# One fused AdaLN layer on one core: set-up reordered, and the slots of the first block rearranged

## The chip, the core and the metric

The kernel runs on 1 core of one Trainium2 chip. A core has five engines with instruction streams of their own: TensorE (PE; its weight loads are PEld), VectorE (DVE), ScalarE (ACT), GpSimd (POOL) and SyncE (SP), which here issues most of the DMA transfers. An engine runs its own instructions in the order in which they are written, and waits on semaphores where an operand comes from another engine or from a transfer. The issue of a transfer is an instruction of such a stream as well: when it has to wait, everything written behind it on that engine waits too.

The metric is device time in microseconds of one execution, the median of several runs.

## The reference

A batch of B = 4 sequences of T = 2048 tokens with D = 512 channels goes through one layer with two halves. Each half is an adaptive layer norm, an operation and a gated residual:

```python
mod = (silu(c) @ wmod).reshape(B, 6, 1, -1)          # sa, ca, ga, sb, cb, gb per sequence
h = layernorm(x) * (1 + ca) + sa
x = x + ga * attn(h)
h = layernorm(x) * (1 + cb) + sb
x = x + gb * ffn(h)
```

`attn` is a damped oscillator with gates that depend on the token. From h come omega (softplus), zeta (sigmoid) and a force F; the state of 2 x 64 numbers then follows a linear recurrence over the 2048 tokens, and the output is `xs @ C.T + h @ D_mat.T`:

```python
z_new = d_t * (S_t * z - DT * A_t * S_t * y)         # A = omega**2, S = 1/(1 + DT**2 A), d = 1 - zeta
y_new = d_t * (DT * S_t * z + S_t * y)
x_new = concatenate([z_new, y_new]) + F_t
```

`ffn` mixes each token with the one before it and has a receptance, a key and a value product, each 512 x 512:

```python
xr = mu_r * x + (1 - mu_r) * x_prev;  xk = mu_k * x + (1 - mu_k) * x_prev
out = sigmoid(xr @ W_r.T) * (square(relu(xk @ W_k.T)) @ W_v.T)
```

All is float32.

## The kernel before

**Units, blocks, slots.** The tokens are cut into pieces of 256 tokens of one sequence: 32 units, numbered so that unit i has block s = i // 4 and sequence b = i % 4. Units 0 to 3 are the first block, one piece of each sequence. Each unit has two halves. `gts[i]` is the gate half: statistics of the raw tokens, the product with the gate weights (`project`), and the delivery of the gates into the maps of its block. `scan(s)` is VectorE's recurrence over the four units of a block; it is a list of steps with costs, and `take(n)` in the program's text emits steps of it up to n microseconds. Its result, the states y, goes by DMA from the maps to a tile of another layout (L414). `fin[i]` is the finish half: the direct product with D and the product with the states (`attend`), the layer norm of the result (`normalize`), transposes and the token mix (`mix`), and then `key`, `receptance` and `value`.

The loop over `fin` (L1203) has one slot per unit. A slot finishes unit i, prepares unit i + 1 (`ahead`) and does gate work of units i + 9 and i + 10. Slots 0 to 3 are written one way (L1206 to L1269), all later ones another way, which the change leaves alone.

**A gate unit's norm.** For units from 4 on, ScalarE computes mean and variance with accumulating activations (`norm`, L187 and L193), GpSimd makes 1/std and std (L197 to L199), `send` writes these 2 KB from SBUF to DRAM (L203, each partition holds 4 numbers), `spread` reads one row back as a broadcast to 128 partitions (L214), and `multiply` (L258, VectorE) scales the projected gates by it. `deliver` then writes them to the maps on ScalarE (L273) and, with `share`, on VectorE (L271). `spread` can be issued only when the write of `send` has landed. Up to gts[7] both are issued by GpSimd, from gts[8] on by SyncE.

**Set-up (L1028 to L1187).** The weights are specialised per sequence: gate weights, and for each sequence b a D matrix scaled by columns: a TensorE product called a pick (`scale_rows`, L122) spreads one row over all partitions, VectorE multiplies it with D into `dg[:, b]` (`d_scaled`, L966), ScalarE scales by rows (`Turn.rows`, L979), TensorE transposes (`Turn.turn`, L988), ScalarE copies it back (`Turn.keep`, L992), and SyncE stores it to DRAM for the later blocks (L798). Before that, `dg[:, 2]` holds the transposed tokens of gts[4] and gts[5], `dg[:, 3]` those of gts[6] and gts[7], so `d_scaled(2)` and `d_scaled(3)` must follow these projects. `fin[b].products()` (L470, L484) forms the direct product of the first block ahead of time and parks it. The steps of `scan(0)` stand between all these on VectorE.

**Buffers that matter.** The raw tokens of the gate units go through a ring of three tiles (`xs`, L159): the second tile of gts[5] takes the first one of gts[4], so its load waits until norm(4) has read it; likewise the second of gts[9] waits for norm(8). The tokens of gts[6] and gts[7] lie in `wr` until the receptance weights are loaded there, `px` is a ring of three PSUM tiles, `pm` and `pt` have two each. `made_early` and `raw_gates` are parts of `wvb`, the place of the value weights.

The order of everything around the change is the order of the program's text: no scheduler moves instructions.

Of the kernel before, what the change touches and what calls it, by code (L numbers as in the profile page):

```python
# [21 lines left out]
P = 128  # L22
# [28 lines left out]
def adaln_layer_kernel(ctx: ExitStack, tc: tile.TileContext, x, x_t, c_t, wmod, w_gate, w_b, b_gate, b_f, c_mat, d_mat,  # L51
# [223 lines left out]
    def scan(s):  # L275
# [123 lines left out]
        def by_batch(q):  # L399


            if q == 0:
                y_of[s] = p2.tile([P, B, W], F32, tag="y", name=f"y_{s}")
            t = [whole[:, i, 1, ts(q, W)] for i in range(2)]
            for i in range(2):
                there = t[i].rearrange("p (c l) -> p l c", l=L)
                if s == 0:
                    nc.scalar.copy(there, parts[:, i, 0, :, q, :])
                else:
                    std = env["std"][:, ts(q, W)].rearrange("p (c l) -> p l c", l=L)  # L410
                    nc.vector.tensor_mul(there, parts[:, i, 0, :, q, :], std)
            for r in range(2):
                for i in range(2):
                    (nc.sync if s else nc.scalar).dma_start(y_of[s][ts(i, M), 2 * q + r, :], t[i][ts(r, M), :])  # L414
# [17 lines left out]
    class Finish:  # L432
# [148 lines left out]
        def mix(self, between):  # L581
            xn, b = self.xn, self.u.b
            mixed = self.mixed = p1.tile([P, 2, KC, W], F32, tag="mixed", name=f"mixed_{self.tag}")
            edge = p2.tile([P, 2, KC], F32, tag="edge", name=f"edge_{self.tag}")
            if self.u.s == 0:
                nc.gpsimd.tensor_copy(edge, first_f[:, b])
            else:
                nc.gpsimd.tensor_tensor(
                    edge, prev_f[:, b], carry[:, b, :].unsqueeze(1).broadcast_to([P, 2, KC]), ALU.mult
                )  # L590
            pts = []
            for g in range(KC // 2):
                pt = ps2.tile([P, 2, W], F32, tag="pt", name=f"pt_{self.tag}_{g}")
                for j in range(2):
                    for n in range(NT):
                        nc.tensor.transpose(pt[:, j, ts(n, P)], xn[:, n, ts(2 * g + j, P)], ident)  # L596
                pts.append(pt)

            for i in (1, 0):
                for k in (0, 2, 1, 3):  # L600
                    pt, m = pts[k // 2][:, k % 2, :], mixed[:, i, k, :]
                    nc.scalar.activation(  # L602
                        m, pt, AF.Identity, bias=mod[:, SB, k, b : b + 1], scale=now_f[:, b, i, k : k + 1]
                    )
                    nc.vector.scalar_tensor_tensor(  # L605
                        m[:, 1:], pt[:, : W - 1], prev_f[:, b, i, k : k + 1], m[:, 1:], ALU.mult, ALU.add
                    )
                nc.gpsimd.tensor_tensor(mixed[:, i, :, 0], mixed[:, i, :, 0], edge[:, i, :], ALU.add)  # L608
                if i == 1:
                    if self.fast:  # L610
                        self.key_sums()

                        nc.gpsimd.tensor_copy(edge[:, 1, 0:1], self.sums[:, 3, 1, W // 2 - 1 :])
                    between()
            for g, pt in enumerate(pts):
                nc.vector.tensor_copy(carry[:, b, 2 * g : 2 * g + 2], pt[:, :, W - 1])
# [5 lines left out]
        def key(self):  # L622
            mixed = self.mixed
            act = self.act = p1.tile([P, KC, W], F32, tag="act", name=f"act_{self.tag}")
            for e in range(KC // 2):
                pk = ps2.tile([P, 2, W], F32, tag="pm", name=f"pk_{self.tag}_{e}")
                for j in range(2):
                    for k in range(KC):
                        nc.tensor.matmul(
                            pk[:, j, :], wk[:, k, ts(2 * e + j, P)], mixed[:, 1, k, :],  # L630
                            start=(k == 0), stop=(k == KC - 1),
                        )
                nc.scalar.activation(act[:, 2 * e : 2 * e + 2, :], pk, AF.Relu)  # L633
                self.squares(e)
# [63 lines left out]
        def token_quarters(self, which):  # L698
            return [[self.mixed[:, which, 2 * k : 2 * k + 2, ts(t, P)] for t in range(2)] for k in range(2)]
# [35 lines left out]
        def receptance(self):  # L735
            mixed = self.mixed
            self.r = []
            for n in range(NT):
                pr = ps2.tile([P, D], F32, tag="pm", name=f"pr_{self.tag}_{n}")
                for k in range(KC):  # L740
                    nc.tensor.matmul(pr, mixed[:, 0, k, ts(n, P)], wr[:, k, :], start=(k == 0), stop=(k == KC - 1))  # L741
                r = p2.tile([P, D], F32, tag="r", name=f"r_{self.tag}_{n}")
                nc.scalar.activation(r, pr, AF.Sigmoid)
                self.r.append(r)
# [114 lines left out]
    mixed_room = p1.tile([P, 2, KC, W], F32, tag="mixed", name="dt_room")  # L859
    dt = mixed_room.rearrange("p i k w -> p (i k w)").rearrange("p (k n) -> p k n", k=KC)  # L860
    dn, wn = wr, wvb[:, 3]
# [108 lines left out]
    class Turn:  # L970
# [19 lines left out]
        def keep(self):  # L990
            for k in (2, 3, 0, 1):
                nc.scalar.copy(self.dst[:, k, :], self.pts[k])  # L992
            keep_in_dram("dg", self.b)
# [96 lines left out]
    gts[4].project()  # L1090
    for i in (6, 7):
        load_transposed(gts[i].u, gts[i].xt)
    gts[4].load()
    weights_to(wn, w_v, nc.sync)
    weights_to(wk, w_k, nc.sync)
# [8 lines left out]
    rowb = mod_rows(wm_gb, "gb", room=px)  # L1104
    rowc = mod_rows(wm_cb, "cb", room=px)
    gts[4].keep_raw()
    gts[5].project(ps3.tile([P, 2, W], F32, tag="px", name="pg_5"))
    gts[4].norm_means()
# [4 lines left out]
    gts[6].project()  # L1113
    turn_d[0].turn()
    turn_d[0].keep()
    pca = scale_rows(2)
    d_scaled(2, pca)
    take(6)
    turn_d[1].rows()
    row = mod_rows(wm_sb, "sb", room=px)  # L1120
# [7 lines left out]
    gts[4].norm_squares()  # L1128
    gts[4].send(nc.gpsimd)
    gts[7].project()  # L1130
    fin[0].products()
    turn_d[1].turn()
    turn_d[1].keep()
    gts[7].keep_raw()
    pca = scale_rows(3)
    d_scaled(3, pca)
    take(100)
    turn_d[2].rows()
# [6 lines left out]
    gts[4].spread(nc.gpsimd)  # L1145
    fin[1].products()
    turn_d[2].turn()
    turn_d[2].keep()
    gts[8].load_t()
    gts[5].norm()  # L1150
    gts[5].send(nc.gpsimd)
    turn_d[3].rows()
    fin[2].products()
    turn_d[3].turn()
    turn_d[3].keep()
    gts[5].spread(nc.gpsimd)
    gts[9].load_t()
    fin[3].products()
# [6 lines left out]
    fin[1].add_products()  # L1165
    c23 = c_rows(2, made_early[0])
    gts[4].multiply()
    gts[6].norm()
    gts[6].send(nc.gpsimd)
    fin[0].attend(lambda: None)  # L1170
    fin[0].normalize()
    gts[8].project()
    gts[4].deliver(share=1)
    gts[8].keep_raw()
    fin[1].shift(nc.vector)
    gts[6].spread(nc.gpsimd)
    fin[0].mix(lambda: None)
    gts[9].project(ps3.tile([P, 2, W], F32, tag="px", name="pg_9"))
# [24 lines left out]
    for i, f in enumerate(fin):  # L1203
        at = i % B
        ahead = fin[i + 1] if i + 1 < len(fin) else None
        if i < 4:  # L1206
            if i == 3:
                take(100)
            fin[i + 2].load()
            gts[i + 10].load()  # L1210
            f.key()
            if i == 0:
                ahead.attend(lambda: None)
                ahead.stats(NT - 1)
                ahead.norm_factors()
            if i == 0:
                gts[6].multiply()
                gts[6].deliver(share=1)
            else:
                norm_send(i + 9)  # L1220
            if i == 3:
                gates(11)
            take(4 if i == 1 else 6)
            if i == 2:
                sums_s(key_weights, quarters_of(wk, True))
            if i == 3:
                sums_t(receptance_weights, quarters_of(wr))
            if i:
                if not ahead.fast:
                    ahead.add_products()  # L1230
                ahead.attend(lambda: take(2))
                ahead.normalize()
            else:
                ahead.norm_apply()
            if i == 0:
                c_scaled(2, c23)
            if i == 1:
                gts[9].multiply()
                gts[9].deliver()
            value_scaled(i)  # L1240
            if i == 3:
                fetch("dg", i + 3)
            if i == 0:
                gts[7].multiply()
                gts[7].deliver(share=1)
                gts[8].norm()
# [4 lines left out]
            if i:  # L1251
                take(5)
            f.receptance()
            ahead.mix(fin[i + 2].shift)
            if i == 0:
                side += scan(1)
                take(0.1)
                take(0.1)
            if i:
                gts[i + 9].load_t()  # L1260
            gts[i + 9].spread()
            f.value(lambda: take(3 if i == 0 else 4), room=px)
            if i < 3:
                ahead.gate_row = ahead.row(1)
# [3 lines left out]
            if i == 1:  # L1268
                gates(10)  # L1269
        else:  # L1270
# [181 lines left out]
```

## Time and profile before

| | us |
|---|---|
| median of 3 runs | 1159.91 (1157.11 to 1160.78) |
| profiled execution, its own time | 1159.07 |
| its span, first to last instruction | 1157.3 |
| PE busy | 1094.4 (95%) |
| DVE busy | 752.1 (65%) |
| ACT busy | 661.4 (57%) |
| POOL busy | 186.6 (16%) |
| mean granted TensorE clock | 0.979 |

The profile is that of one execution, 1.8 us shorter in span than in time. A page of a profile gives busy time by engine, the span in 40 slices, transfers by queue, the chain of work that ended last, and the costliest groups of instructions. The trace behind it can be asked for waits (who waited for whom, total, times, longest), for the timeline of an engine (start, length, instruction, and in brackets the idle time before it and what ended it), and for busy time by stretch. An "SPq" row is the issue of a transfer by SyncE, not the transfer itself.

Landmarks of the execution: the last step of scan(0) ends at 104.6 us; the states of the first block are multiplied from 117.25; the transposes of units 1, 2 and 3 (L596) start at 152.64, 197.03 and 238.30; the key product of unit 3 ends at 256.5.

### The profile page before, as it was taken

How to read it: one execution, taken by the hardware profiler on the slowest of the kernel's cores; microseconds unless marked ns; L12 is line 12 of the kernel's file. 1: busy time of each engine (PE TensorE's matmuls, PEld its weight loads, DVE VectorE, ACT ScalarE, POOL GpSimd, SP SyncE). 2: the span in 40 equal slices, each digit the busy share in tenths (PEclk: the TensorE clock that was granted, in tenths of full speed). 3: DMA queues.
4: the chain of work that ended last, by engine and by line, in shares of the span. 5: the costliest groups of instructions: out<-in, count | busy, mean ns of one | idle time of the engine just before them, and what ended most of it. 6: DMA issues, size and time to landing. Idle time of an engine off the chain costs nothing.

```text
span 1157.3 us, 14456 instructions
## 1 busy us (share of the span) xinstructions
PE 1094.4 (95%) x4692; PEld 733.2 (63%) x4692; DVE 752.1 (65%) x1824; ACT 661.4 (57%) x1366; POOL 186.6 (16%) x379
## 2 busy tenths in 40 slices
PE   7987867889999999999999999999999999999998
PEld 4753533554677766666667766666666665566666
DVE  5647538846777578765886568755876567664444
ACT  1655665443756476657755576657765565435453
POOL 1111220112121112111111011111111011111110
PEclk8999888889999999999999999999999999999999
DMA  9937225455245754577555754576656753444311
GB/s 312 324 128 174 87 78 99 133 160 161 88 161 158 142 162 128 175 226 152 174 168 162 139 168 132 158 238 136 176 168 168 130 175 137 146 155 136 101 55 37
DMA packets 136835, 176.68 MB, mean 153 GB/s; under 512 B 22828, under 2 KB 94764, under 8 KB 129080
## 3 DMA queue, kind: packets, MB, share of 16 engines
q1 hardware_dynamic: 133112, 173.92, 51.9%
q10 hardware_dynamic: 3328, 1.32, 0.4%
q0 software_dynamic: 320, 0.53, 0.4%
q8 instruction: 37, 0.61, 0.2%
q14 instruction: 38, 0.31, 0.1%
HBM read 146.29 MB, written 25.25 MB: 148 GB/s over the span
## 4 chain that ended last, share of the span: by engine, by line
PE 72%; DMA 12%; ACT 7%; DVE 5%; SPq 2%; issue 1%; POOL 1%; ACTq 0%; DVEq 0%; POOLq 0%
PE pv_c L756 15%; PE pd_c L534 12%; PE pxk_c L659 7%; PE pxr_c L659 6%; PE pg L245 5%; DMA xt<-in_x_t_dram 4%; DMA bc<-st 4%; PE pg L235 4%; PE pzk_c L659 4%; PE pzr_c L659 3%; PE pd_c L492 3%; PE pd_c L470 3%; DMA st<-rs 2%; PE pt_c L596 2%; PE pr_c L741 2%; PE pyk_c L659 2%
## 5 line engine op out<-in xcount | busy, mean ns | idle before, releaser
L756 PE MATMUL pv_c<-wvb,act_c 128*128 128x512 f32 (+1 forms) x528 | 227.5, 584 | 0.0
L534 PE MATMUL pd_c<-dg,xt 128*128 128x512 f32 x432 | 206.2, 593 | 0.0
L605 DVE SCALAR_TENSOR_TENSOR mixed_c<-pt_c,prev_f,mixed_c 128x255 f32<-128x255 f32 x256 | 118.2, 481 | 85.3 <-ACT mixed_c L602 85.3
L756 PEld LDWEIGHTS pv_c<-wvb,act_c 128*128 128x128 f32 x528 | 100.6, 192 | 107.2 <-issue 101.5
L602 ACT ACTIVATE mixed_c<-pt_c,mod,now_f 128x256 f32<-128x256 f32 x256 | 130.5, 560 | 25.5 <-DVE mixed_c L605 19.5
L273 ACT ACTIVATE maps<-g,bias 64x256 f32<-64x256 f32 x112 | 83.2, 742 | 75.0 <-DVE g L258 67.5
L534 PEld LDWEIGHTS pd_c<-dg,xt 128*128 128x128 f32 x432 | 74.5, 191 | 55.9 <-issue 55.0
L245 PE MATMUL pg<-xt,wgb 128*128 128x256 f32 x320 | 85.4, 379 | 0.0
L553 ACT ACTIVATE xn_c<-x 128x512 f32<-128x512 f32 x44 | 27.7, 629 | 93.6 <-DVE x L478 89.7
L659 PEld LDWEIGHTS pxk_c<-dg 128*128 128x128 f32 x448 | 58.7, 191 | 26.1 <-issue 24.1
L478 DVE SCALAR_TENSOR_TENSOR x<-pd_c,rs,x 128x512 f32<-128x512 f32 x56 | 41.7, 745 | 48.5 <-PE pd_c L492 48.4
L463 POOL TENSOR_TENSOR x<-x,row 128x1024 f32<-128x1024 f32 x30 | 70.7, 2355 | 3.3 <-DMA row<-col_rows 3.1
L576 ACT ACTIVATE xn_c<-x,mean_c,var_c 128x512 f32<-128x512 f32 x64 | 48.6, 807 | 29.8 <-POOL mean_c L572 29.7
L245 PEld LDWEIGHTS pg<-xt,wgb 128*128 128x128 f32 x320 | 59.2, 190 | 7.2
L659 PE MATMUL pxk_c<-dg 128*128 128x128 f32 x448 | 59.1, 275 | 0.0
L492 PE MATMUL pd_c<-cg,y 128*128 128x512 f32 x112 | 56.3, 593 | 0.0
L659 PE MATMUL pxr_c<-wvb 128*128 128x256 f32 x208 | 53.4, 379 | 0.0
L741 PE MATMUL pr_c<-wr,mixed_c 128*128 128x512 f32 x96 | 44.4, 618 | 6.5 <-ACT act_c L633 6.1
L596 PE MATMUL pt_c<-ident,xn_c 128*128 128x128 f32 x256 | 36.1, 284 | 13.3 <-ACT xn_c L576 13.3
L608 POOL TENSOR_TENSOR mixed_c<-mixed_c,edge_c 128x4 f32<-128x4 f32 x64 | 13.4, 210 | 218.6 <-ACT mixed_c L602 195.3
L759 DVE TENSOR_TENSOR r_c<-pv_c,r_c 128x512 f32<-128x512 f32 (+1 forms) x66 | 44.0, 666 | 6.5 <-PE pv_c L756 6.4
L677 DVE TENSOR_TENSOR act_c<-act_c,pzk_c 128x256 f32<-128x256 f32 x28 | 11.8, 420 | 54.1 <-PE pzk_c L659 53.9
(254 smaller groups left out, 2027.4 us busy)
## 6 DMA issues: line engine op xcount, KB each, us to landing
dg<-dg SPq DMA_DIRECT2D x30, 1024.0 KB, 7.8
xt<-in_x_t_dram SPq DMA_DIRECT2D x112, 256.0 KB, 7.8
wvb<-wv SPq DMA_DIRECT2D x26, 1024.0 KB, 15.0
x<-in_x_dram SPq DMA_DIRECT2D x32, 512.0 KB, 7.0
out_dram<-r_c SPq DMA_DIRECT2D x62, 256.0 KB, 2.0
xs<-in_x_dram SPq DMA_DIRECT2D x54, 256.0 KB, 12.4
row<-col_rows SPq DMA_DIRECT2D x36, 256.0 KB, 11.6
wvb<-in_wmod_dram SPq DMA_DIRECT2D x5, 1024.0 KB, 8.8
```

Of the source, the lines that this page charges most:

```text
L245: nc.tensor.matmul(self.pg[:, i, :], wgb[:, u.b, k, ts(i, P)], self.xt[:, k, :], start=(k == 0), stop=(k == KC - 1))
L273: nc.scalar.activation(there, here, AF.Identity, scale=sign, bias=bias[src, i, b : b + 1])
L463: engine.tensor_tensor(xt, xt, self.shift_row.unsqueeze(1).broadcast_to([P, NT, D]), ALU.add)
L492: nc.tensor.matmul(pc, y_of[u.s][:, u.b, ts(n, P)], cg[:, u.b, :], start=start, stop=True)
L534: nc.tensor.matmul(pds[n], self.h[:, k, ts(n, P)], dg[:, self.at, k, :], start=(k == 0), stop=False)
L576: nc.scalar.activation(self.xn[:, n, :], self.x[:, n, :], AF.Identity, bias=self.mean[:, n : n + 1], scale=self.var[:, n : n + 1],)
L596: nc.tensor.transpose(pt[:, j, ts(n, P)], xn[:, n, ts(2 * g + j, P)], ident)
L602: nc.scalar.activation(m, pt, AF.Identity, bias=mod[:, SB, k, b : b + 1], scale=now_f[:, b, i, k : k + 1])
L605: nc.vector.scalar_tensor_tensor(m[:, 1:], pt[:, : W - 1], prev_f[:, b, i, k : k + 1], m[:, 1:], ALU.mult, ALU.add)
L659: nc.tensor.matmul(to[:, j, :], left[:, k, ts(j, P)], right[:, k, :], start=start and j == k == 0, stop=(k == 1), skip_group_check=True,)
L741: nc.tensor.matmul(pr, mixed[:, 0, k, ts(n, P)], wr[:, k, :], start=(k == 0), stop=(k == KC - 1))
L756: nc.tensor.matmul(pv, act[:, k, ts(n, P)], wvb[:, self.at, k, at], start=(j == 0), stop=(j == KC - 1))
```

## The change

In the set-up, the picks of sequences 2 and 3 move up behind project(4); the D matrix's other copy `dt` gets its room in `wk`, so the load of the key weights moves behind its use; norm(4) moves from two places (its means ahead of turn 0, its squares behind turn 1's rows) to one place behind turn 2; project(6) and project(7) move to stand behind turn 0, one of them in the PSUM ring px; two of the products move later, products(3) behind unit 0's normalize; the four stores of dg move out of `Turn.keep` to one place behind the scan; norm(6) moves behind the mix of unit 0, ahead of norm(7). Half of the transfers of y in the first block go through SyncE instead of ScalarE.

In slots 0 to 2, attend and normalize of the coming unit come first, then key; the mix is split into `turn` (transposes), `mix_part(1)` (for the key) and `mix_part(0)` (for the receptance) with a tile each, and receptance stands between the two parts; the norm, send and spread of gts[i + 9] (in slot 0 of gts[8] and gts[9]) move behind the second part. Slot 3 keeps its order. The core of the diff:

```diff
-                    (nc.sync if s else nc.scalar).dma_start(y_of[s][ts(i, M), 2 * q + r, :], t[i][ts(r, M), :])
+                    (nc.scalar if s == 0 and r else nc.sync).dma_start(y_of[s][ts(i, M), 2 * q + r, :], t[i][ts(r, M), :])
...
-    dn, wn = wr, wvb[:, 3]
+    dn, dt, wn = wr, wk, wvb[:, 3]
...
         def keep(self):
             for k in (2, 3, 0, 1):
                 nc.scalar.copy(self.dst[:, k, :], self.pts[k])
-            keep_in_dram("dg", self.b)
...
     gts[4].project()
+    pcas = [scale_rows(b) for b in range(2, B)]
     for i in (6, 7):
         load_transposed(gts[i].u, gts[i].xt)
     gts[4].load()
     weights_to(wn, w_v, nc.sync)
-    weights_to(wk, w_k, nc.sync)
     gts[5].load()
...
+    weights_to(wk, w_k, nc.sync)
+    rowb = mod_rows(wm_gb, "gb")
+    rowc = mod_rows(wm_cb, "cb")
     gts[4].keep_raw()
     gts[5].project(ps3.tile([P, 2, W], F32, tag="px", name="pg_5"))
-    gts[4].norm_means()
     turn_d[0].rows()
...
-    gts[6].project()
     turn_d[0].turn()
     turn_d[0].keep()
-    pca = scale_rows(2)
-    d_scaled(2, pca)
+    gts[6].project()
+    d_scaled(2, pcas[0])
     take(6)
+    gts[7].project(ps3.tile([P, 2, W], F32, tag="px", name="pg_7"))
     turn_d[1].rows()
...
-    gts[4].norm_squares()
-    gts[4].send(nc.gpsimd)
-    gts[7].project()
-    fin[0].products()
+    gts[7].keep_raw()
     turn_d[1].turn()
     turn_d[1].keep()
-    gts[7].keep_raw()
-    pca = scale_rows(3)
-    d_scaled(3, pca)
+    d_scaled(3, pcas[1])
     take(100)
+    fin[0].products()
     turn_d[2].rows()
...
-    gts[4].spread(nc.gpsimd)
-    fin[1].products()
     turn_d[2].turn()
     turn_d[2].keep()
+    gts[4].norm()
+    gts[4].send(nc.gpsimd)
+    fin[1].products()
+    turn_d[3].rows()
+    turn_d[3].turn()
+    turn_d[3].keep()
+    gts[4].spread(nc.gpsimd)
     gts[8].load_t()
+    fin[2].products()
     gts[5].norm()
     gts[5].send(nc.gpsimd)
...
     fin[1].add_products()
+    for b in range(B):
+        keep_in_dram("dg", b)
     c23 = c_rows(2, made_early[0])
+    gts[5].spread(nc.gpsimd)
+    gts[9].load_t()
     gts[4].multiply()
+    fin[0].attend(lambda: None)
+    fin[0].normalize()
+    fin[3].products()
+    gts[4].deliver(share=1)
+    gts[8].project()
+    gts[8].keep_raw()
+    fin[1].shift(nc.vector)
+    fin[0].mix(lambda: None)
+    gts[9].project(ps3.tile([P, 2, W], F32, tag="px", name="pg_9"))
     gts[6].norm()
     gts[6].send(nc.gpsimd)
     gts[6].spread(nc.gpsimd)
     gts[7].norm()
     gts[7].send(nc.gpsimd)
```

The slots 0 to 2 after the change, whole:

```python
        if i < 3:
            fin[i + 2].load()
            if i:
                gts[i + 9].load_t()
            gts[i + 10].load()
            if i:
                ahead.add_products()
            ahead.attend(lambda: None)
            ahead.normalize()
            f.key()
            if i == 0:
                gts[6].multiply()
                gts[6].deliver(share=1)
                c_scaled(2, c23)
            if i == 1:
                gts[9].multiply()
                gts[9].deliver()
            if i == 2:
                sums_s(key_weights, quarters_of(wk, True))
            take(6)
            value_scaled(i)
            ahead.turn()
            ahead.mix_part(1)
            f.receptance()
            if i == 0:
                gts[7].multiply()
                gts[7].deliver(share=1)
            take(5)
            ahead.mix_part(0)
            ahead.keep_carry()
            fin[i + 2].shift()
            if i == 0:
                side += scan(1)
                take(0.1)
                take(0.1)
                gts[8].norm()
                gts[8].send()
                gts[8].spread()
                gts[9].norm()
                gts[9].send()
            else:
                norm_send(i + 9)
            gts[i + 9].spread()
            f.value(lambda: take(4), room=px)
            ahead.gate_row = ahead.row(1)
            if i == 0:
                gts[8].multiply()
                gts[8].deliver()
            if i == 1:
                gates(10)
```

## The prediction

> **What bounds the kernel now.** I read the busy table by stretch first, then the waits inside the bad stretch, then the chain and two queues' timelines. Units 0 to 3 are the first block; gts[i] and fin[i] are the gate half and the finish half of unit i. All times are us from the span's start.
>
> ```profile
> 55.00:256.50 201.50, 154.37 (x504) 93.13 (x503) 125.03 (x289) 106.02 (x204) 35.22 (x74) 0.90 0.43 117
> 256.50:1100.00 843.50, 839.68 (x3689) 567.22 (x3688) 565.37 (x1392) 508.37 (x1070) 139.66 (x271) 1.00 0.55 157
> ```
>
> Columns are length, then busy PE, PEld, DVE, ACT, POOL, then granted clock, DMA share, GB/s. From 256.5 on TensorE is busy 839.68 of 843.50, so what arrives late there ends late, and nothing is regained. Before it, from 55, TensorE idles 47 us. The change lives in that stretch; its worth is the change of those 47 us. The waits there:
>
> ```profile
> POOL bc L214 <- DMA st<-rs: 27.9, 3, 12.1
> ...
> DVE dg L966 <- PE pca L122: 19.6, 2, 11.2
> ...
> PE pc_c L492 <- DMA y<-maps: 6.9, 1, 6.9
> ```
>
> VectorE waits 19.6 us for two picks (what the change aims at). GpSimd waits 27.9 us for the 2 KB write of the norm rows. The chain shows one such trip ending in VectorE's multiply:
>
> ```profile
> 137.18 12.41 DMA st<-rs
> ...
> 150.17 4.12 DMA bc<-st
> ...
> 154.38 0.70 DVE g L258
> ```
>
> And SyncE's queue shows it twice more:
>
> ```profile
> 163.54 0.38 SPq L798 DMA_DIRECT2D wv<-wvb  x1
> 164.02 0.39 SPq L203 DMA_DIRECT2D st<-rs  x1
> 177.60 0.32 SPq L214 DMA_DIRECT2D bc<-st  x1
> 178.01 0.39 SPq L203 DMA_DIRECT2D st<-rs  x1
> 187.31 0.32 SPq L214 DMA_DIRECT2D bc<-st  x1
> ```
>
> From issuing the write to issuing the read takes 9.3 us when nothing is ahead (178.01 to 187.31; GpSimd's 121.73 to 131.06 the same) and 13.0 to 13.6 with a 1 MB transfer issued beside it (137.18 to 150.17, 164.02 to 177.60). The read lands 3.6 to 4.6 later. So from norm to multiply a trip costs 1.6 (GpSimd) + 9.3 to 13.6 + about 4 = 15 to 19 us. Today norm(8) ends at 159.2 and its multiply runs at 181.53 unwaited: cover is ample.
>
> **Set-up: what the picks give.** The picks of batches 2 and 3 go early: 2 x 0.95 us of PE after project(4). Then d_scaled(2) waits only for project(5) (it overwrites those columns in dg): cols, rows and project shift 1.9, end 54.8, against 60.7 now. d_scaled(3) needs project(6) and (7), moved directly behind the first turn: 56.5 + 1.65 + 3.5 + 3.5 = 65.1, against 80.66. The remaining scan is unchanged, 82.87 to 104.6 = 21.8 plus the 2.3 of d_scaled, so VectorE ends it near 89 instead of 104.6: 15 earlier. Two queues take that back.
>
> ScalarE: its order is keep(0), rows(1), three copies, keep(1), products(0), rows(2), keep(2), norm(4), products(1), rows(3), keep(3), products(2), norm(5), then the copies of y. With 2.05 a keep, 2.9 a rows, 7.0 of PE per products, 1.65 per turn, 2.75 a norm I get keep(1) to 71.0, products(0) 76.8, keep(2) 83.35, norm(4) 86.1, keep(3) 95.75, products(2) 101.5, norm(5) 104.3. So y is copied at 104.3 against 110.97.
>
> SyncE: the second load of gts[5] waits for norm(4)'s square (a buffer ring of three), as now it blocks the queue from 47.2 to 67.3. norm(4) has moved, so it blocks to 85.5. Behind it stand w_k (moved) and col_rows, 10.0 to the first row read, then rows, and c_rows, 6.3 to landing: 104.9. c_scaled and the three x additions follow, 105 to 109.9, with nothing saved against 104.63 to 109.3. y, half of it now on SyncE, lands near 110; attend(0) starts at 110.2 against 117.25, then products(3) (7.1, moved here) and project(8) run on PE while GpSimd waits for st of gts[5] to 117.5 before unit 0's norm factors. Transposes near 124.5, the mixes of unit 0 end at 130.2 against 132.9 (last mixed L605 and L602). Gain so far: 2.7. The four 1 MB stores of dg, now behind y in one go, plus c_rows and xt of gts[9], are 5 MB: at 340 GB/s (the 80 to 100 stretch's rate at full share) 15 us from 109. That is beside PE's 22 us up to project(9), so nothing; at half that rate project(9) waits 8 us, hidden because the next wait lasts to 161.
>
> **First slot: two trips in series.** gts[6] and gts[7] are normed only after the mix, and GpSimd's order is send(6), spread(6), norm(7), send(7), spread(7), and only then the norm factors of unit 1. norm(6) ends 132.9, send 134.55, spread 147.5 (13.0: w_r's 1 MB goes out beside it, as today), then 0.6 + 1.55, send(7) 149.6, + 9.35 = spread(7) at 159.0, factors to 160.55, xn, unit 1's transposes at 161.6. Today: 152.64. That is 9.0 late, and the receptance of unit 0, which today fills that gap, now stands behind the transposes.
>
> **Slots 1 and 2: the multiply comes straight after its norm.** norm(8) moves from 156.6 to behind both mixes and the softening: transposes 164.1, receptance 7.4 (its first part at the low clock; the page's slices show 8 here) 171.5, sigmoid, gates(7) 1.5, second mix 2.5, Abs to Ln 5.0 = 181.2. SyncE then holds: xs of gts[9] waits for norm(8)'s first square (183.3), the shift row of unit 2 stands behind it and lands at 188.4, and GpSimd shifts x (2.36) before norm(8)'s own small work. send(8) 192.4; between 9.35 and 13.6 I take 11 as wv's 1 MB went 4 us before: spread 203.5, landed 207. On VectorE multiply(8) stands ahead of unit 2's additions and of half of scan(1); it would be reached at 187, so it waits 20. Then 0.7 + 1.2 + 3.6 + GpSimd 1.3 gives unit 2's transposes at 215.1; today 197.03. Late by 18.
>
> Slot 2 repeats it. multiply(9) 217.5, value_scaled(1) to 226.8, first mix 229, three scan steps, second mix 237.2, norm(10) to 239.9, shift, xs and wv ahead, send(10) 241.4, 13.2 (1 MB directly ahead) + 0.3 + 3.6 = 258.5. VectorE would be at multiply(10) at 245.3. Additions to 261.2, ScalarE's gates and statistics to 265.1, GpSimd 1.7, transposes of unit 3 at 267.8; today 238.30. Then receptance 7.4, value 7.1, key 7.1 and the transposes 2.4: key(3) ends 291.8 against 256.5, late by 35.3 (today the receptance ran before the transposes). Last, y of the second block stands on SyncE behind spread(11): 300.5 against TensorE's need at 298.8, 1.7 more. The rest I cost at nothing. Two tiles instead of one add no instruction and free nothing that is waited for. attend ahead of key puts 1.9 us of PE first, but unit 1's factors wait for spread(7) anyway; in return ScalarE reaches key(0)'s relu only after xn, 162.3, beside transposes and receptance, which last to 171.5. The earlier xt loads of gts[10] and gts[11] land long before their projects. mod_rows moves from px to pm in PSUM, whose buffers were emptied at 42. From unit 3 on the order is as before.
>
> Sum: 35.3 + 1.7 = 37.0 later than the profiled execution, whose time is 1159.07 (span 1157.3 + 1.8): 1196.1. That execution is 0.84 below the median of 1159.91, so 1196 to 1197; I say 1196.
>
> The Trainium skill's page "DMA: Bandwidth & Descriptors", section "Anatomy of one DMA — SWDGE (gpsimd) path", gives about 2 us fixed per DMA plus bytes, for this 2 KB write as for any. The rows above show 8.8 to 12.4 us to landing for it, so the rows decide; by the page the four trips below one another would be some 40 us shorter in all and key(3) would end some 3 us earlier than now, 1156 (an estimate from that page). The same page's "Rules for kernel authors" says to issue a DMA early and wait on it late; the changed order does the reverse for gts[8] and gts[10].
>
> **Rivals.**
> - Faster: the trips of gts[8] and gts[10] are hidden, so TensorE runs through from unit 1's transposes at 161.6. Its work to the end of key(3) is 77.6 (transposes 2.4, receptance 7.5, then eight stages of 7.1, project 3.5, two state products of 1.9, two sets of transposes of 1.8), ending 239.2, 17 earlier: 1142. VectorE has 62 us of work there, which fits. It decides if norm to multiply takes under 3 us in slot 1 and under 6 in slot 2; no trip in the trace took under 14.
> - Half: slot 1 waits as worked out, slot 2's trip is covered (a statement order I misread, or a short landing). From 215.1 TensorE needs 52.5: 267.6, 11 late: 1170.
> - Worse: the 5 MB stores are slow, st of gts[5] and gts[6] land 4 to 6 later each, and the later writes all take 13.6: 37 + 9 to 16: 1205 to 1212.
> - The scan still waits: d_scaled(2) for project(5) 2.4, d_scaled(3) for project(7) 1.5. So the aim is met but for 4 us; it moves the total nowhere, since ScalarE and SyncE end later.
>
> **How the numbers follow.** Forecast 0.62, half 0.17, worse 0.13, faster 0.07, no change 0.01. With every write at 9.3 the forecast's own low end is 37 - 3.7 - 1.7 - 3.8 = 28, and with the set-up 5 better 23: its own range is 1182 to 1205. The half rival bounds the range below at 1170, the worse one above at 1212. A difference of 0.3% (3.5 us) is about what these runs can tell from none: slower 0.92, same 0.01, faster 0.07.
>
> **What would show it.** VectorE's wait for picks gone, its scan over near 89, but c_scaled near 105. GpSimd's wait at spread(6) 9 to 13 long, unit 1's transposes near 161. VectorE waiting some 10 to 20 us at L258 for bc, twice; TensorE idle of about 20 us three times before 270, and its total idle from 55 to the steady part about 84 instead of 47. Wrong if the multiplies of gts[8] and gts[10] show no wait, or if unit 2's transposes come before 200.

## The result and the profile after

The changed kernel takes 1201.53 us (median of 4 runs, 1200.39 to 1207.3) against 1158.51 of the kernel before beside it: ratio 1.0382, 95% interval 1.0341 to 1.0423. It is slower, inside the predicted range and 5.5 us above the predicted 1196. The profiled execution took 1200.39 us, 41.3 more than the profiled one of before (1159.07); the sum of the prediction was 37.0.

Busy time by stretch, changed kernel (columns as in the prediction: length, PE, PEld, DVE, ACT, POOL, clock, DMA share, GB/s):

```profile
55.00:288.70 233.70, 151.34 (x520) 93.43 (x519) 127.16 (x289) 107.90 (x212) 36.71 (x75) 0.82 0.38 99
288.70:310.20 21.50, 14.07 (x37) 7.43 (x36) 4.81 (x8) 6.77 (x14) 1.07 (x3) 0.84 0.51 142
310.20:1142.00 831.80, 828.34 (x3655) 560.74 (x3654) 561.34 (x1385) 502.24 (x1057) 137.13 (x269) 1.00 0.55 157
```

The first stretch again ends with the key product of unit 3. TensorE is idle for 82.4 of its 233.7 us, where before it was idle for 47.1 of 201.5. The second runs to the receptance of unit 3, and TensorE is idle for another 7.4 there. From 310.2 on it is busy for 828.3 of 831.8 at a granted clock of 1.00, so nothing of the loss comes back.

The waits of VectorE, TensorE and GpSimd from 55 to 300, changed kernel (total, times, longest):

```profile
PE pt_c L596 <- ACT xn_c L576: 57.9, 7, 25.7
DVE g L258 <- DMA bc<-st: 54.0, 5, 18.5
...
POOL bc L214 <- DMA st<-rs: 41.2, 4, 10.7
...
DVE cg L1006 <- DMA c_rows<-col_rows: 13.4, 1, 13.4
...
PE pg L235 <- DMA xt<-in_x_t_dram: 11.1, 1, 11.1
...
PE pc_c L492 <- DMA y<-maps: 6.7, 1, 6.7
...
DVE dg L973 <- PE pg L235: 3.9, 2, 2.2
```

The 19.6 us that VectorE waited for picks are gone, and 3.9 for `project` came in their place. The new waits are larger: 54.0 for the norm rows at the multiply, where before had one of 5.5, and 13.4 for `c_rows`, which swallows nearly all of the 15 us by which the scan is earlier. TensorE's wait at the transposes for the coming unit's norm rose from 13.3 to 57.9; its wait for y of the first block is as before, 6.7 against 6.9, and the 11.1 for the input of gts[9] come back below.

The chain through one row trip, from four timelines of the changed kernel. SyncE's queue with the rows of gts[8] and gts[9] (their norms are written at the end of slot 0, and they are waited for while TensorE is in slot 1):

```profile
188.59 0.38 SPq L807 DMA_DIRECT2D wv<-wvb  x1
191.71 0.38 SPq L203 DMA_DIRECT2D st<-rs  x1
203.70 0.32 SPq L214 DMA_DIRECT2D bc<-st  x1
204.11 0.39 SPq L203 DMA_DIRECT2D st<-rs  x1
212.67 0.32 SPq L214 DMA_DIRECT2D bc<-st  x1
```

VectorE's multiplies of gts[8], gts[9] and gts[10] (in brackets the idle time before, and what ended it):

```profile
206.62 0.69 DVE L258 TENSOR_TENSOR g<-wvb,bc 128x512 f32<-128x512 f32 x1 [18.52 <-DMA bc<-st]
...
217.68 0.69 DVE L258 TENSOR_TENSOR g<-wvb,bc 128x512 f32<-128x512 f32 x1 [5.70 <-DMA bc<-st]
...
255.12 0.69 DVE L258 TENSOR_TENSOR g<-pg,bc 128x512 f32<-128x512 f32 x1 [9.68 <-DMA bc<-st]
```

And TensorE's first transposes of units 1, 2 and 3:

```profile
162.09 0.47 PE L596 MATMUL pt_c<-ident,xn_c 128*128 128x128 f32 x1 [12.29 <-ACT xn_c L576]
...
213.85 0.47 PE L596 MATMUL pt_c<-ident,xn_c 128*128 128x128 f32 x1 [25.70 <-ACT xn_c L576]
...
264.11 0.47 PE L596 MATMUL pt_c<-ident,xn_c 128*128 128x128 f32 x1 [18.94 <-ACT xn_c L576]
```

GpSimd, ahead of the first row (the shift of unit 2's x):

```profile
188.00 2.34 POOL L463 TENSOR_TENSOR x<-x,row 128x1024 f32<-128x1024 f32 x1 [10.71 <-DMA row<-col_rows]
```

Read them together. The norm of gts[8] ends on ScalarE at 184.6, but its row leaves only 7 us later: GpSimd's small work for it is written behind the shift of unit 2's x, which waits for a transfer of its own. The row of gts[8] leaves at 191.71, SyncE may read it back at 203.70, VectorE has stood for 18.52 us when it lands, and the additions to unit 2's x stand behind that multiply on VectorE. So unit 2 reaches the transposes at 213.85, after TensorE has been idle for 25.70. Unit 3 repeats it with the row of gts[10]. Before, the three sets of transposes started at 152.64, 197.03 and 238.30.

The last part of the loss lies at the second block's states, in SyncE's queue:

```profile
283.05 0.38 SPq L203 DMA_DIRECT2D st<-rs  x1
293.82 0.32 SPq L214 DMA_DIRECT2D bc<-st  x1
294.23 0.86 SPq L771 DMA_DIRECT2D out_dram<-r_c  x2
295.14 0.45 SPq L448 DMA_DIRECT2D row<-col_rows  x1
295.68 7.20 SPq L414 DMA_DIRECT2D y<-maps  x8
```

and on TensorE:

```profile
291.94 3.60 PE L470 MATMUL pd_c<-dg,xt 128*128 128x512 f32 x8
302.96 2.05 PE L492 MATMUL pd_c<-cg,y 128*128 128x512 f32 x2 [7.43 <-DMA y<-maps]
304.80 4.63 PE L470 MATMUL pd_c<-dg,xt 128*128 128x512 f32 x8
```

The eight copies of y are written behind the reading of gts[11]'s row. SyncE stands from 283.4 to 293.8, and TensorE, ready at 295.5, starts at 302.96. The products after that wait run slower for a moment: eight products of L470 take 4.63 after it and 3.60 ahead of it.

### The profile page after: what moved, and what is told of

It is laid out like the page before. It is cut to its first block, busy times and chain, and to the rows that moved or that the text cites. A ratio compares the mean times of both kernels' runs of the same rounds, so it can differ in the third digit from the quotient of the medians.

```text
span 1198.6 us, 14487 instructions
## 1 busy us (share of the span) xinstructions
PE 1093.3 (91%) x4692; PEld 732.8 (61%) x4692; DVE 754.2 (63%) x1824; ACT 660.8 (55%) x1366; POOL 185.6 (15%) x379
## 4 chain that ended last, share of the span: by engine, by line
PE 69%; DMA 8%; DVE 4%; ACT 4%; issue 1%; POOL 1%; SPq 0%; DVEq 0%; POOLq 0%
PE pv_c L765 16%; PE pd_c L534 13%; PE pxk_c L668 7%; PE pxr_c L668 7%; PE pg L245 5%; PE pzk_c L668 4%; PE pzr_c L668 3%; DMA st<-rs 3%; PE pd_c L492 3%; PE pr_c L750 3%; PE pt_c L596 2%; DMA bc<-st 2%; PE pyr_c L668 2%; PE pyk_c L668 2%; DMA xt<-in_x_t_dram 2%
## 5 line engine op out<-in xcount | busy, mean ns | idle before, releaser
L765 PE MATMUL pv_c<-wvb,act_c 128*128 128x512 f32 (+1 forms) x528 | 225.1, 579 | 1.4 <-DVE wvb L1011 1.4
L596 PE MATMUL pt_c<-ident,xn_c 128*128 128x128 f32 x256 | 37.0, 288 | 57.9 <-ACT xn_c L576 57.9
L553 ACT ACTIVATE xn_c<-x 128x512 f32<-128x512 f32 x44 | 27.6, 628 | 89.7 <-DVE x L478 89.7
L576 ACT ACTIVATE xn_c<-x,mean_c,var_c 128x512 f32<-128x512 f32 x64 | 48.6, 807 | 49.9 <-POOL mean_c L572 49.8
L478 DVE SCALAR_TENSOR_TENSOR x<-pd_c,rs,x 128x512 f32<-128x512 f32 x56 | 41.7, 745 | 52.1 <-PE pd_c L492 52.1
L596 PEld LDWEIGHTS pt_c<-ident,xn_c 128*128 128x128 f32 x256 | 31.7, 148 | 64.5 <-ACT xn_c L576 60.3
L610 POOL TENSOR_TENSOR mixed_c<-mixed_c,edge_c 128x4 f32<-128x4 f32 x64 | 12.9, 202 | 255.3 <-issue 222.1
L769 DVE TENSOR_TENSOR r_c<-r_c,x 128x512 f32<-128x512 f32 (+1 forms) x66 | 46.7, 708 | 2.3
```

What stands on the lines that cost most here:

```text
L576: nc.scalar.activation(self.xn[:, n, :], self.x[:, n, :], AF.Identity, bias=self.mean[:, n : n + 1], scale=self.var[:, n : n + 1],)
L765: nc.tensor.matmul(pv, act[:, k, ts(n, P)], wvb[:, self.at, k, at], start=(j == 0), stop=(j == KC - 1))
L769: nc.vector.tensor_add(r[:, at], r[:, at], xt[:, n, at])
```

## The experiments

All edits are of the changed kernel. Each ratio is to the kernel before, run in the same group of runs. The medians of before in the four groups were 1158.81, 1155.31, 1151.73 and 1154.12, so ratios are compared across groups, and not times. The changed kernel stands at 1.0382.

**e1, the norms of the slots back behind the key.**

```diff
             f.key()
+            if i == 0:
+                gts[8].norm()
+                gts[8].send()
+                gts[8].spread()
+                gts[9].norm()
+                gts[9].send()
+            else:
+                norm_send(i + 9)
             if i == 0:
                 gts[6].multiply()
...
                 take(0.1)
-                gts[8].norm()
-                gts[8].send()
-                gts[8].spread()
-                gts[9].norm()
-                gts[9].send()
-            else:
-                norm_send(i + 9)
             gts[i + 9].spread()
```

> The changed kernel with one thing undone: in slots 0 to 2 the norms and sends of gts[8], gts[9], gts[10] and gts[11] stand behind the key again instead of behind the second mix. Theory (the row trips of gts[8] and gts[10] hold VectorE at their multiplies): VectorE's waits of 18.5, 5.7 and 9.7 us at the multiplies go, unit 1's transposes stay near 162, unit 2's come near 200 instead of 213.85, unit 3's near 238 instead of 264.11, and the second block's states no longer wait 7.4 us; 1155 to 1168 us. Rival (the order inside the slot, attend ahead of key and receptance behind the transposes, costs by itself): at most 5 us come back, 1195 or more.

Measured: 1166.09 us, ratio 1.0062 (1.004 to 1.0084). In slot 0 the norms now stand directly behind the key; the kernel before has them there later, behind the multiply of gts[7]. The waits for the rows at L258 fall from 54.0 to 10.7, of which 8.3 belong to gts[6], and the transposes start at 163.24, 200.97 and 238.16. The trips themselves are hardly shorter:

```profile
172.77 0.39 SPq L203 DMA_DIRECT2D st<-rs  x1
183.99 0.33 SPq L214 DMA_DIRECT2D bc<-st  x1
```

That is 11.2 us from writing to reading back, against 12.0. The trip lies beside the mix of unit 1 and the value product of unit 0 now, and the shift of unit 2's x no longer stands ahead of it. So the place of the norm in the slot, and nothing else that was done to the slots, costs most of the 43 us.

**e2, the norm of gts[6] back around unit 0's attention.**

```diff
     gts[4].multiply()
+    gts[6].norm()
+    gts[6].send(nc.gpsimd)
     fin[0].attend(lambda: None)
...
     fin[1].shift(nc.vector)
+    gts[6].spread(nc.gpsimd)
     fin[0].mix(lambda: None)
...
-    gts[6].norm()
-    gts[6].send(nc.gpsimd)
-    gts[6].spread(nc.gpsimd)
     gts[7].norm()
```

> The changed kernel with one thing undone: norm(6) and its send stand ahead of unit 0's attend again and its spread ahead of the mix, so GpSimd has one row trip, not two in series, ahead of unit 1's norm factors. Theory: unit 1's transposes come near 150 instead of 162.09, everything behind moves with them, 1188 to 1192 us. Rival (the wait for the tokens of gts[9], 11.1 us at project(9), is what makes unit 1 late): transposes move by under 3 us and the time stays within 4 of 1201.

Measured: 1194.1 us, ratio 1.0305 (1.028 to 1.033). The gain is there, but it falls short of the expected time by 2 us. The reason stands in TensorE's timeline of this run:

```profile
141.66 6.26 PE L235 MATMUL pg<-xt,wgb 128*128 128x256 f32 x16 [12.91 <-DMA xt<-in_x_t_dram]
...
156.38 1.04 PE L596 MATMUL pt_c<-ident,xn_c 128*128 128x128 f32 x8
```

The transposes of unit 1 no longer wait at all. What is late instead is the input of gts[9], a wait that the prediction had at up to 8 us and hidden. With the row early it is no longer hidden, and the transposes come at 156.4 instead of about 150.

**e3 and e4, each half of the change alone.** e3 has the changed set-up, with slots 0 to 3 as the kernel before has them; its core:

```diff
-        if i < 3:
+        if i < 4:
...
-            ahead.attend(lambda: None)
-            ahead.normalize()
             f.key()
...
+                norm_send(i + 9)
...
+            f.receptance()
+            ahead.mix(fin[i + 2].shift)
```

e4 has the changed slots, with the set-up up to the loop (and the stores in `keep`) as the kernel before has it. Both keep the changed queue for y; e3 keeps the mix in two tiles, e4 the room of `dt` in `wk`. The core of e4:

```diff
     gts[4].project()
-    pcas = [scale_rows(b) for b in range(2, B)]
...
+    pca = scale_rows(2)
+    d_scaled(2, pca)
...
     gts[4].multiply()
+    gts[6].norm()
+    gts[6].send(nc.gpsimd)
     fin[0].attend(lambda: None)
```

> The changed set-up with the slots of the kernel before (the mix in two tiles kept, since it is called by both). Theory: scan(0) over near 89.7 as in the changed kernel, unit 1's transposes near 162 instead of 152.64, later waits of the old slots absorb little: 6 to 10 us above the kernel before, 1164 to 1169. Rival (the set-up gains what it was meant to, and the slots alone lose): under 1155.

> The changed slots with the set-up of the kernel before (only the room of dt is that of the changed kernel). Theory: unit 1's transposes near 151, the waits at the multiplies of gts[8] and gts[10] as in the changed kernel, 30 us above the kernel before, 1186 to 1193. Rival (the loss comes from the set-up's pile-up of transfers): within 8 us of the kernel before.

Measured: the set-up alone 1167.68 us, ratio 1.0081 (1.0052 to 1.011); the slots alone 1191.13 us, ratio 1.0269 (1.0241 to 1.0297). The losses of 0.0081 and 0.0269 sum to 0.0350 against 0.0382 for both, so they add within their intervals. The slots' two waits at the transposes are nearly the same from either start, 26.06 and 19.16 in e4 against 25.70 and 18.94. They hardly depend on how late the set-up is.

**e5, both moves of norms undone.** The edits of e1 and e2 together.

> The changed kernel with both moves of norms undone: the norms and sends of gate halves 8 to 11 behind the key of slots 0 to 2 (as in the run that gave 1166.1), and the norm, send and spread of gate half 6 back around unit 0's attention (as in the run that gave 1194.1). Theory: the two row trips are terms of one sum, so the gains of 35.4 and 7.4 add: 1201.5 - 42.8 = 1158.7, range 1154 to 1163, unit 1's transposes at about 156 and unit 3's at about 231. Rival (the slots' loss is only a follow-on of the late start, so that either undoing alone brings all there is): 1164 to 1168, no better than the first of the two.

Measured: 1154.77 us, ratio 0.9992 (0.9981 to 1.0003), unit 1's transposes at 155.78 and unit 3's at 229.56. The two undoings add, and the rest of the change (picks early, the scan free of TensorE, attend ahead of key, two mix tiles, stores behind the scan) is together worth nothing that can be told from zero. (The norms of gts[8] and gts[9] stand where e1 has them, so this is not the slot 0 of the kernel before.)

**e6, the last term alone.** The copies of y of the second block by ScalarE's queue.

```diff
-  (nc.scalar if s == 0 and r else nc.sync).dma_start(y_of[s]...
+  (nc.scalar if s == 1 or (s == 0 and r) else nc.sync).dma_start(y_of[s]...
```

> The changed kernel, with the eight copies of y in the second block issued by ScalarE's queue in place of SyncE's, which is where the last spread of the changed kernel blocks (SyncE stands from 283.4 to 293.8 at gate half 11's row, and y is issued at 295.7). Theory (SyncE's wait for a row holds up y, and TensorE waits 7.4 us for y): the wait at the second block's first products goes, 1193 to 1197. Rival (y lands late because its maps are late, or the time is taken again by the value weights behind it): 1199 to 1203.

Measured: 1190.94 us, ratio 1.0308 (1.0282 to 1.0334), by the ratios 8.5 us under the changed kernel (0.0074 of 1155.31). TensorE has no wait for y there any more:

```profile
294.52 1.02 PE L492 MATMUL pd_c<-cg,y 128*128 128x512 f32 x2
```

So SyncE's wait for a row really holds up the transfers written behind it, and they were on the path.

**e7 and e8, the stores of dg back behind their turns.** e7 is the changed kernel with this edit; e8 has e5's edits too.

```diff
         def keep(self):
             for k in (2, 3, 0, 1):
                 nc.scalar.copy(self.dst[:, k, :], self.pts[k])
+            keep_in_dram("dg", self.b)
...
-    for b in range(B):
-        keep_in_dram("dg", b)
     c23 = c_rows(2, made_early[0])
```

> The changed kernel with the four stores of dg put back right behind each turn of dg (ScalarE's copies), where before had them, in place of all four after the scan. TensorE's wait of 11.1 us for the transposed input of gate half 9 then shortens or goes, since that load no longer stands behind the stores. Theory (the wait is hidden, as unit 1's transposes wait for gate half 6's row anyway): 1199 to 1204, unit 1's transposes still at 160 to 163. Rival (the late stores are the price of the set-up's new order): 1190 to 1196.

> Both moves of norms undone, and the four stores of dg back behind their turns. With gate half 6's row early the input of gate half 9 set the time of unit 1's transposes (156.4, after a wait of 12.9). Theory: with that load earlier too, unit 1's transposes come at 149 to 154 and the kernel gains 2 to 7 on the run with the norms alone: 1151 to 1158, at or under the kernel before (1158.5). Rival (another wait, ScalarE's own work ahead of the norm of unit 1, is as late): within 1.5 of the run with the norms alone.

Measured: e7 1215.0 us, ratio 1.0525 (1.0505 to 1.0546); e8 1169.33 us, ratio 1.0135 (1.0112 to 1.0159). Both are some 16 us worse than without the edit, and neither theory had that. SyncE's queue in e7:

```profile
85.50 0.39 SPq L829 DMA_DIRECT2D wk<-in_w_k_dram  x1
85.98 0.46 SPq L807 DMA_DIRECT2D dg<-dg  x1
86.49 0.44 SPq L1029 DMA_DIRECT2D col_rows<-room  x1
102.24 1.29 SPq L448 DMA_DIRECT2D row<-col_rows  x3
...
118.19 2.12 SPq L115 DMA_DIRECT2D xt<-in_x_t_dram  x2
```

and the same place in the changed kernel:

```profile
86.34 0.39 SPq L829 DMA_DIRECT2D wk<-in_w_k_dram  x1
86.77 0.51 SPq L1028 DMA_DIRECT2D col_rows<-room  x1
91.52 1.30 SPq L448 DMA_DIRECT2D row<-col_rows  x3
```

With the 1 MB store between them, the 24 KB write of `col_rows` lets the read behind it go after 15.8 us and not after 4.8. The copies of y on the same engine are issued at 120.40 and not at 106.20, and TensorE waits 27.7 us for y of the first block instead of 6.7. The load of gts[9]'s input no longer stands behind the stores and lands 4.9 us after its issue in place of 20.1, and TensorE does not wait for it. But it is issued at 128.15 and not at 114.48, and TensorE is later itself, so that is worth nothing beside it. So the late place of the stores is a part of the change that helps the new set-up. The Trainium skill's page "DMA: Bandwidth & Descriptors" (section "Queues, rings and completion order") has it that a transfer's completion signal lands only after every earlier write from the same DMA engine; a small write that counts as done only when the large one ahead of it is done would fit that. It would not by itself say why the read goes only at 102.24, when the trace shows no traffic from 95 to 102. That stays open.

**e9 and e10, the stores later still.** On top of e5, e9 puts them behind the load of gts[9]'s input (shown), and e10 puts those of sequences 0 and 1 there and the other two behind `gates(10)` in slot 1.

```diff
     gts[5].spread(nc.gpsimd)
     gts[9].load_t()
+    for b in range(B):
+        keep_in_dram("dg", b)
     gts[4].multiply()
```

> All norms back (the run that equalled before, ratio 0.9992), and the four 1 MB stores of dg moved one place later still, behind the load of gate half 9's transposed input. In that run the input was issued at 119.2 and landed at 141.9, behind the stores, and TensorE stood 16.4 us for it ahead of unit 1. Theory (a transfer issued behind 4 MB waits for them, and the wait is on the path of unit 1): the wait falls under 5 us, unit 1's transposes come at 142 to 149 instead of 155.8, and the ratio to before is 0.989 to 0.996. Rival (the loads issued behind the stores, receptance weights and inputs of the next gate halves, become late in its place): ratio 0.998 to 1.004.

> As the run with all norms back and the stores behind gate half 9's input, but only two of the four stores there and the other two at the end of slot 1. Theory: 2 MB fewer stand ahead of the receptance weights and of the inputs of gate halves 8 and 9, so it is 0 to 4 us better than the run with all four there, ratio 0.986 to 0.995. Rival (the two stores in slot 1 take the place in front of another row or input there): 0 to 5 us worse than that run.

Measured: e9 1150.46 us, ratio 0.9991 (0.9982 to 1.0); e10 1149.82 us, ratio 0.9981 (0.9969 to 0.9993). In e9 TensorE's wait of 16.4 us for the input is gone and unit 1's transposes come at 150.44, 5.3 earlier than in e5, yet unit 3's come at 225.62, only 3.9 earlier, and the ratio is that of e5. So the ratio lies in the rival's range, although the wait went as the theory said. The traces show the step; e9's ratio does not. e9 and e5 ran in different groups, whose kernels before differ by 3.6 us, as much as the step, so whether it is worth something is not settled. e10's ratio misses its theory's range as well, and its 0.1% against e9 is within the two intervals. It is the one version whose whole interval lies under the kernel before, by 0.2%, less than the 0.3% that the prediction called tellable.

**e11 and e12, receptance ahead of the coming unit's transposes.** e11 on top of e10, e12 on the changed kernel.

```diff
+            f.receptance()
             ahead.turn()
             ahead.mix_part(1)
-            f.receptance()
```

> As the run with all norms back and the four stores of dg split (ratio 0.9981), and in slots 0 to 2 the receptance products are issued ahead of the coming unit's transposes and not behind them. In that run TensorE stood 6.0, 9.3 and 7.5 us for the coming unit's norm while the 7 us of receptance, which needs nothing of it, were queued behind. Theory (TensorE's order is what costs there, once the rows are early): up to 7 us of each wait is filled, less what the next key waits for the mix; 5 to 18 us, ratio 0.983 to 0.994. Rival (VectorE and ScalarE set the length of a slot, and the wait moves to the key behind the mix): ratio 0.996 to 1.003.

> The changed kernel with that one edit alone: receptance ahead of the coming unit's transposes in slots 0 to 2. There TensorE stands 12.3, 25.7 and 18.9 us at the transposes, more than the 7 us of receptance. Theory (the row trip sets the length of a slot: softening, send, spread, multiply, norm, transposes, mix, softening again, and receptance is not in that ring): the waits shrink by 7 each but the transposes come no earlier, 162 / 214 / 264 within 3; the time moves by 0 to -6 us, ratio 1.032 to 1.039. Rival (TensorE's work in a slot adds to the trip): 7 us in each slot, ratio 1.018 to 1.026.

Measured: e11 1157.13 us, ratio 1.0028 (1.0019 to 1.0037); e12 1207.45 us, ratio 1.0463 (1.0441 to 1.0485). Against e10 and the changed kernel that is 0.5% and 0.8% slower, where both theories had a gain or nothing. e11 lies in its rival's range, but not by the rival's mechanism (the key's wait for the mix is 5.3 us there and was 5.0), and e12 lies outside both ranges. The products written earlier find a wait of their own. TensorE in e12:

```profile
217.93 9.37 PE L750 MATMUL pr_c<-wr,mixed_c 128*128 128x512 f32 x16 [28.62 <-ACT act_c L642]
```

and ScalarE in e12:

```profile
215.79 1.52 ACT L576 ACTIVATE xn_c<-x,mean_c,var_c 128x512 f32<-128x512 f32 x2 [2.67 <-POOL mean_c L572]
217.22 0.57 ACT L642 ACTIVATE act_c<-pk_c 128x512 f32<-128x512 f32 x1
```

Receptance needs a PSUM tile of the ring of two that the key holds, and the key's Relu (L642) that frees it stands on ScalarE behind the coming unit's normalization (L576), since attend and normalize were written ahead of key. So receptance waits for the row of gts[8] just as the transposes did, and the transposes of unit 2 now come behind it, at 227.13 instead of 213.85. In e11 receptance waits for the same Relu twice, 19.9 us together. The ring that the theory had drawn was right about the row and wrong about receptance standing outside it.

## Why the prediction came out right, step by step

The sign, the range and nearly all places were right, two of the places with luck.

| step | predicted | measured |
|---|---|---|
| scan(0) ends | 89 | 89.7 |
| `d_scaled` waits for `project` | 2.4 + 1.5 | 3.9 in all |
| `c_scaled` runs at | 105 | 103.0 |
| unit 1's transposes | 161.6 | 162.1 |
| VectorE's wait at multiply(8), its run | 20, at 207 | 18.5, at 206.6 |
| unit 2's transposes | 215.1 | 213.9 |
| multiply(10) | 258.5 | 255.1 |
| unit 3's transposes | 267.8 | 264.1 |
| key(3) ends, late by | 35.3 | 32.1 |
| y of the second block | 1.7 | 9.6 |
| sum | 37.0 | 41.7 |

- **Set-up.** The aim is met and worth nothing by itself, as worked out: `c_rows` holds `c_scaled`. That it does so near the forecast time is in part luck: the write of `col_rows` could be read after 4.8 us and not after 10.0, and `c_rows` was there 10.2 us after its issue (92.86 to 103.04) and not after 6.3. Unit 1's place is luck too: from write to read, the trip of gts[6] was forecast at 13.0 us and took 11.0 (134.96 to 145.93), that of gts[7] was forecast at 9.35 and took 11.5 (148.10 to 159.64). The two errors cancel; the rule behind them, 13 us with a 1 MB transfer beside the write and 9.3 without, did not hold. e3 puts the set-up's loss at 0.8%, and e2, which moves only the norm of gts[6], takes as much back in the changed slots (1.0382 to 1.0305). So there the step "GpSimd's order is send(6), spread(6), norm(7), send(7), spread(7)" carries it. In e3's old slots no run takes it apart: TensorE waits 9.8 us for the input of gts[9] there and 3.2 at unit 1's transposes. "At half that rate project(9) waits 8 us, hidden because the next wait lasts to 161": the wait was 11.1, and it was hidden by the row of gts[7] alone; e2 and e5 uncover it as 12.9 and 16.4.
- **Slots.** "Late by 18" for unit 2 measured 16.8. In slot 2 the term "13.2 (1 MB directly ahead)" was mis-sized: the write was issued 2.1 us behind that store and the read could go after 9.9 us (240.31 to 250.20), near the 9.3 that the prediction took for a row with nothing ahead. That is 3.3 of the 3.7 us by which unit 3 was early.
- **The last term.** "1.7 more" failed by 7.9 us, and it is the step that makes the sum 4 us too small. Counted from unit 3's transposes, TensorE was ready for y when forecast (31.4 us behind them, forecast 298.8 - 267.8 = 31.0), but y came 38.9 us behind them (264.11 to 302.96) where the forecast had 300.5 - 267.8 = 32.7. That makes the wait 7.4 and not 1.7. The other 2.1 are the products behind that wait: the granted clock is 0.50 from 303 to 305 and 1.00 from 307 to 309. The prediction names SyncE's wait at spread(11) as the cause and gives 300.5 without its terms, so which of them was short can't be told. In the run the row of gts[11] could be read 10.8 us after its write (283.05 to 293.82), and issuing the eight copies took 7.2 more. e6, which takes this step out, gains 8.5.
- **Cost at nothing.** "ScalarE reaches key(0)'s relu only after xn, 162.3, beside transposes and receptance" held as long as receptance stood behind the transposes; e12 shows what it hides.
- **Rivals.** The faster one needed a trip of under 3 us; the shortest write of a row in the changed trace took 8.6 (204.11 to 212.67). "Half" fails by multiply(10)'s wait of 9.7, "worse" because the rows of the slots were written in 8.6 to 12.0 us and not all in 13.6. The rows of the trace decided rightly. By the figure of the Trainium skill's page "DMA: Bandwidth & Descriptors" (section "Anatomy of one DMA — SWDGE (gpsimd) path"), about 2 us fixed per transfer, the sum was 1156, an estimate; that fit is for transfers issued by GpSimd, as the rows of gts[6] and gts[7] are, and these took 10.4 and 11.0 us to land.

## What to carry to other kernels

An operand that makes a round trip through DRAM has to be started a whole trip ahead of its use, counted in the work of the engine that consumes it: here 9 to 12 us for writing 2 KB, plus 3 to 6 for reading it back. Moving its producer "next to where it is used" to free one engine puts the trip on the path of all of them, and every issue or instruction that is written behind the waiting one is late too. Undo such a change one move at a time: 43 us of loss were two moves of a norm, and the dozen other edits around them were worth nothing together, though one of them, the late stores, is worth 16 us to the new set-up (e7, e8).

## What was not expected of the hardware

- A 1 MB store issued 0.5 us ahead of a 24 KB write held back the read behind that write by 11 us (15.8 against 4.8, e7); with the same store 0.4 us ahead in the kernel before, the read went after 10.5 (67.73 to 78.24). For a 2 KB row it was 9.9 us with such a store 2.1 us ahead (slot 2 of the changed kernel), 12.0 with one 3.1 us ahead (slot 1) and 10.8 with one 0.6 us ahead (the row of gts[11]), against 13.6 with one 0.5 us ahead in the kernel before and 8.6 to 11.5 with none in the changed kernel. Size and distance alone do not tell it.
- After TensorE's wait of 7.4 us eight products took 4.63 us in place of 3.60, and the eight transposes of a unit take 2.2 us behind a wait (0.47 and 1.76) and 1.04 without one. The granted clock from 55 to 288.7 is 0.82, against 0.90 in that part before. So a wait costs more than its length: 2.1 us more in the last one.
- ScalarE took 10.4 us to issue the eight copies of y in e6, where SyncE took 7.2, and that did not show in the time, since they no longer stood behind a row.
